# Windowed attention in tiles of 128 tokens of one batch, on small array tiles, with plain values and a new order of issue

## The chip, the cores and the metric

The kernel runs on one core of a Trainium2 chip. Five engines of that core work side by side, each through its own queue in order: TensorE (PE: matrix products; PEld is its loading of weights), VectorE (DVE), ScalarE (ACT), GpSimd (POOL) and SyncE (SP, which here only starts transfers). The metric is device time in microseconds. Before the change it is 1421.82 us, the median of 3 runs (1421.61 to 1422.27).

## The reference

x has 4 batches of 256 tokens with 128 features. Eight layers follow one another: cross attention and feed-forward, four times, each added to x with a gate. The change lies in the first two. The first (L0 cross attention) has 16 heads of 64. The second (L0 feed-forward) is a small transformer of its own, six depths of windowed attention and a gated feed-forward:

```python
for i in range(DEPTH):      # 6
    x = attn_layer(shift_tokens(x), Wqkv[i], q_scale[i], k_scale[i], Wo[i]) + x
    x = ffn_layer(shift_tokens(x), ln_g[i], ln_b[i], W1[i], b1[i], W2[i], b2[i]) + x

def attn_layer(x, Wqkv, qs, ksc, Wo):
    q, k, v = heads(x @ Wqkv)                # 16 heads of 64
    q = l2norm(q) * qs;  k = l2norm(k) * ksc
    q = q * cos * scale + rotate_half(q) * sin * scale
    k = k * cos / scale + rotate_half(k) * sin / scale
    # windows of 32 queries, each with the 64 keys of its own and the previous window
    sim = where(mask, -big, einsum('bhwie,bhwje->bhwij', q, k2) * 8.0)
    out = einsum('bhwij,bhwje->bhwie', softmax(sim), v2)
    return merge(out) @ Wo
```

`shift_tokens` delays the upper 64 features by one token, within a batch. The feed-forward is a layernorm, a product to 2 x 341 columns, a * gelu(gate), and a product back.

## The kernel before

The program has three parts. `front` holds the first layer and the preparation of the weights of depth 0, `l0_ffn` the six depths, `tail` the other six layers. In each, every piece of work has a name, and a list (`ORDER_A`, `ORDER_L0`, `ORDER`) says in which order the pieces are given to the engines, so each engine's order is written out by hand. PSUM has eight banks of 128 x 512; `psum` hands them out in rings by tag (`k.psb`: in `l0_ffn` two for the projections "mm", one each for the other tags). Buffers in SBUF come in rings as well.

Products that must be exact are made of three: a number is split in two parts of type fp32r, high and low, and `mm3` (L274, its three products L276 to L278) adds high x high, high x low and low x high. Other products are float32; one float32 product stands in the profile as two records of TensorE, a transpose as one.

**First layer** (`l0_xattn`, L670). By batch and pair of heads: projections of q and k, scores (`head`, op "s": `mm3` of a head's 64 features on 64 rows of the array, 128 queries, 256 keys, twice), maximum on DVE (L768), exponential on ACT (L774), normalising on POOL (L777), transposes (L784), the product with the values, the output projection.

**Six depths** (`l0_ffn`, L890). A tile of work (`tile_ops`, L1006) is one window of 32 tokens of all 4 batches, so 128 rows; a depth has eight, which follow each other because a window needs the keys and values of the one before. A tile does this:

- `x_in` (L1018 to L1021) gathers the window out of x (`xp`, 4 batches of 257 columns), with the shift, by two copies, and takes the high part; `x_lo` the low part on POOL.
- `tab_d` and `tab_m` load the rotary table of the window and multiply it by the depth's scales.
- `proj` (P): q and k in four groups of 512 columns; `square` and `norm` for the l2 norm; `cos` (L1050), `sin` (L1056), `add` (L1059) for the rotation; `scale` (L1072); `rsqrt_seed` (L878, L879: Ln and Exp on ACT) and `newton` on DVE for the inverse norm.
- `trans` (L1077) transposes, `evac` puts q into a block-diagonal buffer `qbd` (L1084: two heads beside each other, zeros between, each half by its own copy) and k into `kT` (L1087).
- `val`: not the values but the values already multiplied by Wo. `weight_ops` makes these folded weights U for each depth (`mm_u`, L959; `hi_u`, L964; `lo_u`, L967). 16 heads x 128 columns are four groups of 512. `val_e` (L1098) evicts, `val_d` moves them by four transfers each into the layout of keys.
- `score` and `score_h`: a mask product of 128x512 in bf16 (L1118), then 8 products (L1126) with 128 rows of `qbd` and 64 columns, on two column tiles of the array, twice.
- `smax` (L1135), `ssub` (L1138), `sexp` (L1142), `ssum` (L1146), `snorm` (L1151), then transposes (L1157) and their eviction (L1161).
- `out_mm` (L1170): P times folded values, on four column tiles of 32, added up over heads in one bank; `out_e`, one transpose, and `out_r` (L1190) adds x.

**Feed-forward** (`group_ops`, L1206): four groups of 64 tokens x 4 batches a depth, from `fx` (two gathering copies, L1215, L1216) through the layernorm, the six products, Gelu on ACT (with a load of its table before it and of the exponential's after it) and the residual (L1293).

Of the kernel before, what the change touches and what calls it, by code (L numbers as in the profile page):

```python
# [58 lines left out]
def shape_constants():  # L59
# [14 lines left out]
    rot = np.zeros((128, 8, 4, 64), f32)  # L74
    for b in range(4):
        for w in range(8):
            rot[32 * b:32 * b + 32, w] = tabs[:, 32 * w:32 * w + 32].transpose(1, 0, 2)
    i = np.arange(32)
    mask = np.zeros((128, 64), f32)
    prev = np.where(i[None, :] >= i[:, None], 0.0, NEG)  # L80
    cur = np.where(i[None, :] <= i[:, None], 0.0, NEG)
    for b in range(4):
        mask[32 * b:32 * b + 32, :32] = prev
        mask[32 * b:32 * b + 32, 32:] = cur
    sel = np.zeros((18, NMC * 128), f32)
    for e in range(9):
# [6 lines left out]
        "rot": rot.reshape(128, -1), "mask": mask, "sel": sel,  # L93
# [5 lines left out]
def lay_out(inp):  # L99
# [15 lines left out]
    def blockdiag(w):  # L115
        r = np.zeros((8, 128, 2, 128), np.float32)
        w = w.reshape(8, 2, 64, 128)
        r[:, :64, 0] = w[:, 0]
        r[:, 64:, 1] = w[:, 1]
        return c(r.transpose(1, 0, 2, 3).reshape(128, 2048))  # L120

# [3 lines left out]
    o["f_wvT"] = c(W[:, :, 2048:].transpose(0, 2, 1).reshape(6, 8, 128, 128).transpose(0, 2, 1, 3).reshape(6, 128, 1024))  # L125
    o["f_wo"] = np.stack([blockdiag(A("L0_ffn_Wo")[i].reshape(16, 64, 128)) for i in range(6)])
# [103 lines left out]
def ring(k, pool, tag, bufs):  # L230
    """Pools in k.rings hand out the buffers of a tag in turn."""
    if bufs == 1 or pool not in k.rings:
        return tag, bufs
    n = k.turn[pool, tag] = k.turn.get((pool, tag), -1) + 1
    return f"{tag}.{n % bufs}", 1


def psum(k, tag, shape=(128, 512)):
    k.n += 1
    tag = tag if tag in k.psb else "p"  # L240
    tag, bufs = ring(k, k.ps, tag, k.psb[tag])
    return k.ps.tile([128, 512], F32, name=f"ps{k.n}", tag=tag, bufs=bufs)
# [22 lines left out]
def split(k, hi, lo, src, e_hi, e_lo):  # L265
    """hi + lo == src, each in float32r."""
# [14 lines left out]
def rsqrt(k, pool, y, x, tag):  # L281
    """y = x ** -0.5 elementwise for small positive x, by three Newton steps from the exponent's halving."""
# [10 lines left out]
def rstd(k, pool, out, var, eps):  # L293
    """out = (var + eps) ** -0.5 on [128, n] tiles."""
# [5 lines left out]
def ln_group(k, pool, src_tok, nt, eps, want_tok, out_eng=None):  # L300
    """Layernorm without affine of nt token tiles given in PSUM or SBUF [128, nt, 128]."""
# [14 lines left out]
class Flow:  # L316
    """Work in pieces, each with a name; ORDER says in which order the engines get them."""
# [23 lines left out]
def lazy(k, pool, shape, tag, bufs=1, dtype=F32):  # L341
    """A tile taken from its ring by the first piece of work that touches it."""
# [9 lines left out]
def newton_steps(V, y, x, t):  # L352
    """Three Newton steps of y() towards x() ** -0.5."""
# [5 lines left out]
def seed(V, y, x):  # L359
    """y close to x ** -0.5, from the halving of the exponent."""  # L360
# [5 lines left out]
xd.0 as.0 aw.0.0 aw.0.1 aw.0.2 aw.0.3 aw.0.4 aw.0.5 aw.0.6 aw.0.7 aw.0.8 aw.0.9 aw.0.10 an.0 au.0 ch.1 zero ch.0 WKd.0  # L366
WQd.0 WKh.0 cl.0 WKl.0 xd.1 WQh.0 as.1 ah.0 aw.1.0 WQl.0 Dwo aw.1.1 al.0 aw.1.2 bq.0.1 bq.0.0 bh.0.1.0 bh.0.1.1
bl.0.1.0 Dmb bh.0.0.0 wud.0 bh.0.0.1 bl.0.1.1 mb.0 bl.0.0.0 bq.0.3 WVd.0 WVd.1 bh.0.3.0 mb.1 bl.0.0.1 s.0.2 WVh.0
m.0.2.0 s.0.1 aw.1.3 s.0.0 m.0.2.1 m.0.1.0 bh.0.3.1 Dbvrow bl.0.3.1 s.0.3 w2d WVh.1 x.0.2 m.0.1.1 bl.0.3.0 x.0.1 z.0.2
WVl.0 aw.1.4 m.0.0.0 aw.1.5 m.0.0.1 xd.2 wsd bq.0.2 bh.0.2.0 bh.0.2.1 x.0.0 v.0.0.0 wum.0 m.0.3.0 WVl.1 ve.0.0.0 z.0.1  # L370
wuh.0 v.0.1.0 n.0.2 m.0.3.1 t.0.2 wud.2 bl.0.2.1 n.0.1 WKd.1 bl.0.2.0 z.0.0 ve.0.1.0 DxT wul.0 n.0.0 s.0.6 x.0.3
m.0.6.0 aw.1.6 WKh.1 z.0.3 e.0.2 t.0.1 m.0.6.1 WQd.1 s.0.5 t.0.0 WQh.1 WKl.1 m.0.5.0 n.0.3 s.0.4 v.0.0.1 e.0.1 e.0.0
o.0.0 x.0.6 aw.1.7 m.0.5.1 s.0.7 WQl.1 as.2 m.0.4.0 x.0.5 z.0.6 t.0.3 m.0.4.1 bq.0.4 cl.1 aw.2.0 bq.0.5 ve.0.0.1 z.0.5
aw.2.1 x.0.4 m.0.7.0 m.0.7.1 bq.0.6 oe.0.0 bh.0.4.0 aw.1.8 bh.0.4.1 y.0.0 e.0.3 z.0.4 o.0.1 bh.0.5.0 aw.1.9 bl.0.4.0
n.0.5 bl.0.4.1 t.0.5 v.0.1.1 n.0.6 n.0.4 bh.0.6.0 bh.0.6.1 w1d.0 w1h.0 bh.0.5.1 aw.2.2 bl.0.6.0 x.0.7 aw.1.10 aw.2.3
bl.0.5.0 wqd.0 an.1 t.0.6 oe.0.1 bl.0.5.1 bl.0.6.1 aw.2.4 z.0.7 e.0.5 ve.0.1.1 s.0.9 aw.2.5 m.0.9.0 m.0.9.1 e.0.6
t.0.4 aw.2.6 s.0.8 s.0.12 wqd.1 m.0.8.0 m.0.12.0 aw.2.7 n.0.7 e.0.4 m.0.8.1 x.0.9 aw.2.8 v.1.0.0 au.1 xd.3 s.0.10
aw.2.9 ah.1 z.0.9 t.0.7 m.0.12.1 o.0.2 aw.2.10 x.0.8 ve.1.0.0 m.0.10.0 al.1 m.0.10.1 s.0.11 z.0.8 x.0.12 w1l.0 n.0.9
t.0.9 oe.0.2 v.1.1.1 z.0.12 bq.1.0 e.0.7 n.0.8 bq.0.7 wqh.0 e.0.9 x.0.10 m.0.11.0 s.0.13 z.0.10 m.0.11.1 as.3 bh.1.0.0
o.0.3 bq.1.1 ve.1.1.1 bh.0.7.0 aw.3.0 bh.0.7.1 y.0.1 bh.1.0.1 bl.1.0.0 bl.0.7.0 aw.3.1 t.0.8 bl.0.7.1 wql.0 bl.1.0.1  # L380
x.0.11 n.0.12 aw.3.2 t.0.12 aw.3.3 s.0.15 m.0.13.0 bh.1.1.0 e.0.8 n.0.10 aw.3.4 oe.0.3 z.0.11 y.0.2 m.0.13.1 aw.3.5
# [288 lines left out]
def l0_xattn(k, op, pool):  # L670
# [159 lines left out]
    for b in range(4):  # L830
        batch(b)


class Early:
    """The weights of depth 0, prepared in a flow."""

    def __init__(self, op):
# [1610 lines left out]
```

## Time and profile before

| what | value |
|---|---|
| median of the runs | 1421.82 us |
| span of the profiled execution | 1416.4 us (5.4 us of the median lie outside it) |
| PE busy | 1280.0 us, 90%, 11538 matmul records |
| DVE busy | 1162.2 us, 82% |
| ACT busy | 1016.9 us, 72% |
| POOL busy | 799.8 us, 56% |
| first stage, up to | 203 us |
| six depths, up to | 1089 us |

A row for an engine counts the time in which at least one of its instructions runs. Matmuls overlap: an instruction of TensorE lasts some 0.28 us from its start until its last result is written, while the next starts much sooner. What a matmul costs in a busy queue is therefore the spacing of the starts, which the view in order of time shows. The same holds for ACT and DVE to a smaller degree. PEclk is the share of TensorE's full clock that was granted.

### The profile page before, as it was taken

The numbers are of one execution on the slowest core, as the hardware profiler recorded it, in microseconds if no ns is written. First come the engines' busy times: TensorE is split into PE (matmuls) and PEld (weight loads), VectorE is DVE, ScalarE is ACT, GpSimd is POOL, SyncE is SP. The second block draws the span as 40 slices with busy tenths as digits, with TensorE's granted clock in tenths as the row PEclk, the third lists the DMA queues.
The fourth block names the chain that finished last, engine by engine and source line by source line (L and its number), as shares of the span: only waits on it lengthen the run. The fifth ranks groups of instructions, "written<-read, shape, count | busy, mean of one in ns | idle before, by whom it ended". The sixth has DMA issues, their size and how long they took to land. (4 is left out here: it accounts for less than half of the span.)

```text
span 1416.4 us, 32751 instructions
## 1 busy us (share of the span) xinstructions
PE 1280.0 (90%) x11538; PEld 926.2 (65%) x11538; DVE 1162.2 (82%) x3086; ACT 1016.9 (72%) x2408; POOL 799.8 (56%) x987
## 2 busy tenths in 40 slices
PE   5999987889999899999999998999995978899896
PEld 4777755667777677777777766777773733555444
DVE  6867667888899989888899898989864885778777
ACT  5766748888888778888788878888782634446871
POOL 4434547867787867777787777867640111631221
PEclk9999989999999999999999999999996968999676
DMA  5000002234333333333333432332231110201200
GB/s 181 27 20 4 9 17 74 78 80 107 82 93 94 91 84 95 85 88 93 89 102 82 123 83 76 81 89 74 68 74 39 33 47 15 71 0 45 83 1 15
DMA packets 79433, 95.24 MB, mean 67 GB/s; under 512 B 21513, under 2 KB 47793, under 8 KB 79271
## 3 DMA queue, kind: packets, MB, share of 16 engines
q1 hardware_dynamic: 79271, 93.16, 24.5%
q8 instruction: 92, 1.51, 0.5%
q14 instruction: 70, 0.57, 0.1%
HBM read 40.14 MB, written 2.62 MB: 30 GB/s over the span
## 5 line engine op out<-in xcount | busy, mean ns | idle before, releaser
L1126 PEld LDWEIGHTS ps<-fkT,qbd 128*64 128x64 f32 x3072 | 102.7, 138 | 40.4 <-issue 31.7
L1126 PE MATMUL ps<-fkT,qbd 128*64 128x64 f32 (+1 forms) x3072 | 124.1, 227 | 2.4 <-ACT fkT L1087 2.3
L1084 ACT COPY qbd<-ps 64x512 f32<-64x512 f32 x192 | 111.1, 579 | 9.8 <-PE ps L1077 8.3
L777 POOL TENSOR_TENSOR P<-P,pz 128x512 f32<-128x512 f32 x64 | 66.1, 1041 | 86.6 <-DVE pz L776 63.9
L774 ACT ACTIVATE P<-P,pm 128x256 f32<-128x256 f32 x128 | 64.0, 505 | 10.0 <-DVE pm L768 9.7
L768 DVE CUSTOM_DVE_ANT_0 P<-ps,mb 128x256 f32<-128x256 f32 x128 | 50.5, 417 | 22.6 <-PE ps L784 11.2
L2188 ACT ACTIVATE l3P<-ps,l3m 128x256 f32<-128x256 f32 x128 | 58.7, 489 | 10.8 <-PE ps L2207 3.9
L1087 ACT COPY fkT<-ps 128x512 f32<-128x512 f32 x96 | 56.5, 588 | 10.7 <-PE ps L1077 10.4
L1277 DVE SCALAR_TENSOR_TENSOR fge<-ps,cols,fge 114x256 f32<-114x256 f32 x72 | 34.3, 477 | 20.4 <-PE ps L278 10.1
L588 PE MATMUL ps<-ident,ln_xn 128*128 128x128 f32 x72 | 18.9, 340 | 31.8 <-DVE ln_xn L582 31.4
L2179 DVE TENSOR_REDUCE l3m<-ps 128x2 f32<-128x512 f32 x64 | 41.9, 681 | 6.1 <-PE ps L2173 4.3
L725 ACT ACTIVATE qk<-ps,cols 128x256 fp32r<-128x256 f32 x64 | 27.6, 472 | 22.3 <-PE ps L278 21.1
L1270 ACT ACTIVATE fge<-ps,cols 114x256 f32<-114x256 f32 x72 | 34.4, 478 | 9.9 <-PE ps L278 9.2
L588 PEld LDWEIGHTS ps<-ident,ln_xn 128*128 128x128 f32 x72 | 10.3, 158 | 46.8 <-DVE ln_xn L582 21.6
L572 POOL TENSOR_TENSOR ln_h<-ln_x,half 128x2 f32<-128x2 f32 x16 | 3.1, 195 | 66.4 <-DVE ln_x L570 66.0
L276 PE MATMUL ps<-qk 64*128 64x256 f32 x128 | 40.0, 326 | 0.2 <-DVE V L744 0.2
L726 DVE SCALAR_TENSOR_TENSOR qk<-ps,cols,qk 128x256 fp32r<-128x256 f32 x64 | 29.0, 476 | 13.0 <-ACT qk L725 12.9
L784 PE MATMUL ps<-ident,P 128*128 128x128 f32 x256 | 38.4, 279 | 0.4 <-POOL P L777 0.2
L1282 PE MATMUL ps<-fge,fw 114*128 114x256 f32 x144 | 37.2, 395 | 0.7 <-DVE fge L1277 0.7
L1118 PE MATMUL ps<-mk,idb 128*128 128x512 bf16 (+1 forms) x96 | 35.8, 373 | 0.9 <-DVE fP.1_3795_16221 L1138 0.3
L2016 ACT ACTIVATE ma<-ps,cols 128x512 f32<-128x512 f32 x26 | 18.0, 692 | 23.5 <-PE ps L2049 13.6
L277 PE MATMUL ps<-qk 64*128 64x256 f32 x128 | 34.3, 279 | 0.0
(5111 smaller groups left out, 5312.6 us busy)
## 6 DMA issues: line engine op xcount, KB each, us to landing
fwo<-in_f_wo_dram SPq DMA_DIRECT2D x24, 256.0 KB, 3.8
wst<-in_f_wqk_dram SPq DMA_DIRECT2D x24, 256.0 KB, 2.9
fwv<-in_f_wvT_dram SPq DMA_DIRECT2D x24, 128.0 KB, 2.6
w1st<-in_f_w_dram SPq DMA_DIRECT2D x18, 114.0 KB, 2.6
l3K<-dn SPq DMA_DIRECT2D x4, 512.0 KB, 4.0
l3Q<-do SPq DMA_DIRECT2D x8, 256.0 KB, 3.3
wst<-in_m_w_dram SPq DMA_DIRECT2D x6, 256.0 KB, 2.7
fw<-in_f_w_dram SPq DMA_DIRECT2D x6, 171.0 KB
```

Of the source, the lines that this page charges most:

```text
L276: mm(out, lh, rh, start=start, stop=False, **kw)
L768: V.tensor_tensor_reduce(w.P[:, i], w.sp[:, i], mb[:, i], -0.125, 3.0e38, ALU.add, ALU.min, w.m[:, i:i + 1])
L774: nc.scalar.activation(w.P[:, i], w.P[:, i], AF.Exp, scale=-1.0, bias=w.m[:, i:i + 1], accum_out=z()[:, i:i + 1])
L777: op("n", b, h)(lambda: nc.gpsimd.tensor_tensor(w.P, w.P, bc(z().unsqueeze(2), [128, 2, BT]), ALU.mult))
L784: nc.tensor.transpose(w.pt[:, kc, i * 128:(i + 1) * 128], w.P[:, i, kc * 128:(kc + 1) * 128], k.ident)
L1084: nc.scalar.copy(k.qbd[w % 2][r, 4 * j:4 * j + 4, :, par], p[r].rearrange("p (a b t) -> p a b t", a=4, b=4))
L1087: nc.scalar.copy(k.kT[:, s.slot, 4 * jj:4 * jj + 4], p.rearrange("p (a b t) -> p a b t", a=4, b=4))
L1118: nc.tensor.matmul(s4, k.idb, bc(mkv.unsqueeze(1), [128, 8, nb, 32]), start=True, stop=False, skip_group_check=True)
L1126: nc.tensor.matmul(sp[64 * b2:64 * b2 + 64, pr], k.qbd[w % 2][:, pr, 2 * bb + b2].rearrange("p a t -> p (a t)"), k.kT[:, ks, pr, 2 * bb + ...
L1282: nc.tensor.matmul(s.y, d.w2[:, c], s.ge[:, c], start=(c == 0), stop=(c == 2))
L2179: V.tensor_reduce(w.m, w.sp, AX.X, ALU.max, negate=True)
L2188: nc.scalar.activation(P[kc, hp][:, a], w.sp[:, a], AF.Exp, bias=w.m[:, a:a + 1], accum_out=u.z[:, h:h + 1])
```

## The change

The six depths are cut in another way. A tile is now 128 successive tokens (four windows) of one batch; a depth has two for each of four batches. x is kept already shifted, one buffer per batch (`k.X`), so that no gathering is needed, and the feed-forward works on one batch. The order lists are new for the first stage and the six depths; the banks of PSUM are given out by two written lists (`BANKS_A`, `BANKS_L0`) there. `tail` keeps its list.

- Scores: for each of 4 windows, 8 head pairs and 2 heads, one product of 64 rows, 32 queries and 64 keys on a tile of 64x32 of the array; the mask comes from 8 products of 64 rows and 512 columns on the same tiles. Even and odd heads have a bank each.
- The factor 8 is in q's table; the negative maximum is the bias of the exponential, which is one instruction per head (8 for a bank), and the subtraction goes.
- Values are projected plainly (two groups of 512 columns), the folded weights and `mm_u`, `hi_u`, `lo_u` go; PV is 64 products of 64 rows, 64 columns of values and 32 queries on 64x64 tiles, and the output projection follows as eight products (O) after two evictions (Ce).
- The rotary tables stay in SBUF and are multiplied by the scales twice a depth.
- q's transposes are evicted whole, as k's are. A table of ACT is loaded where the function needs another one than was loaded last (`table`).
- In the first stage, the scores of the two heads of a pair are made in turn, on rows 0 to 63 and 64 to 127, in two banks.

```diff
 # l0_xattn
-                    mm3(k, w.sp[:, i], t[r, 0, q], t[r, 1, q], t[r, 2], t[r, 3])
+                    for n, (u, v) in enumerate(((0, 2), (0, 3), (1, 2))):
+                        for j, w in enumerate(sp):
+                            r = slice(64 * j, 64 * j + 64)
+                            nc.tensor.matmul(w.sp[:, i], t[r, u, q], t[r, v], start=(n == 0), stop=(n == 2),
+                                             tile_position=(64 * j, 0), skip_group_check=True)
...
+def table(k, name):
+    if k.table != name:
+        k.table = name
+        k.nc.scalar.preload_act_table_set(name)
...
 # values
-        uh, ul = d.U[hh]
-        mm3(k, s.vp[hh], s.xh, s.xl, uh.rearrange("p r i o -> p (r i o)"), ul.rearrange("p r i o -> p (r i o)"))
+                mm3(k, s.vp[r], xh()[:, ts], xl()[:, ts], d.v[r][0], d.v[r][1])
...
+                for i in range(4):
+                    src = s.vt[r][32 * i:32 * i + 32].rearrange("p (a f) -> p a f", a=8)
+                    nc.sync.dma_start(vu[g]()[cur, i], src)
+                    if g == 0 and i == 0:
+                        nc.sync.dma_start(vu[0]()[nxt, 0], src)
+                    if i < 3:
+                        nc.sync.dma_start(vu[g]()[nxt, i + 1], src)
+                    elif g == 0:
+                        nc.sync.dma_start(vu[1]()[nxt, 0], src)
...
 # scores
-                nc.tensor.matmul(sp[64 * b2:64 * b2 + 64, pr], k.qbd[w % 2][:, pr, 2 * bb + b2].rearrange("p a t -> p (a t)"),
-                                 k.kT[:, ks, pr, 2 * bb + b2], start=False, stop=True, skip_group_check=True,
-                                 tile_position=(0, 64 * b2))
+            for i in range(4):
+                for par in range(2):
+                    r = slice(64 * par, 64 * par + 64)
+                    nc.tensor.matmul(s.sp[par][32 * i:32 * i + 32], k.sel[r, 1 if g == 0 and i == 0 else 0],
+                                     bc(k.mk[r].unsqueeze(1), [64, 8, 64]), start=True, stop=False,
+                                     tile_position=(64 * par, 32 * i), skip_group_check=True)
+            for pr in range(8):
+                for i in range(4):
+                    for par in range(2):
+                        r = slice(64 * par, 64 * par + 64)
+                        c = 128 * g + 32 * i
+                        nc.tensor.matmul(s.sp[par][32 * i:32 * i + 32, pr], qT()[r, pr, 32 * i:32 * i + 32], kT()[r, pr, c:c + 64],
+                                         start=False, stop=True, tile_position=(64 * par, 32 * i), skip_group_check=True)
...
 # softmax
-        V.tensor_tensor(views(s.P[bb])[1], s.sp[bb].rearrange("p h (c m) -> p h c m", c=nb),
-                        bc(s.mx[bb].unsqueeze(2).unsqueeze(3), [128, 8, nb, 32]), ALU.subtract)
-        nc.scalar.activation(views(s.P[bb])[0], views(s.P[bb])[0], AF.Exp, scale=8.0)
+                for pr in range(8):
+                    nc.scalar.activation(P()[:, pr], s.sp[par][:, pr], AF.Exp, bias=mx()[:, pr:pr + 1])
...
 # PV and output projection
-                nc.tensor.matmul(s.y[32 * b:32 * b + 32, :128], s.PT[b // 2][:, g % 2, c, q0:q0 + 32], v[:, b, g],
-                                 start=(g == 0 and c == 0), stop=(g == 3 and c == nb - 1), tile_position=(0, 32 * b),
-                                 skip_group_check=True)
+            s.o = [psum(k, "o").rearrange("p (m q) -> p m q", m=4) for _ in range(2)]
+            for m in range(4):
+                for i in range(4):
+                    q = slice(32 * i, 32 * i + 32)
+                    for par in range(2):
+                        for r in range(2):
+                            kk = slice(64 * r, 64 * r + 64)
+                            nc.tensor.matmul(s.o[r][64 * par:64 * par + 64, m, q], vu[g]()[kk, i, 4 * par + m], s.PT[par]()[kk, m, q],
+                                             start=True, stop=True, tile_position=(64 * r, 64 * par), skip_group_check=True)
+        for r in range(2):
+            op("Ce", l, b, g, r)(lambda r=r: nc.scalar.copy(o()[:, r], s.o[r]))
+            s.y = psum(k, "y")[:, :128]
+            for pr in range(8):
+                nc.tensor.matmul(s.y, d.wo[:, pr], o()[:, pr % 2, pr // 2], start=(pr == 0), stop=(pr == 7))
+            for h in range(2):
+                p, c = halves(h, 128 * g, 128)
+                V.tensor_tensor(u.x1()[p, c], s.y[p], X()[p, c], ALU.add)
...
 # feed-forward
-        nc.vector.scalar_tensor_tensor(d.x2[:, :, c], s.y.rearrange("p (b i) -> p b i", b=4), col(k, "f_b2", l),
-                                       d.x1[:, :, c], ALU.add, ALU.add)
+        for h in range(2):
+            p, c = halves(h, 0, 256)
+            nc.vector.scalar_tensor_tensor(x2()[p, c], s.y[p], col(k, "f_b2", l, 64 * h, 64 * h + 64), x1()[p, c], ALU.add, ALU.add)
```

## The prediction

> **What bounds the kernel now.** The profiled execution spans 1416.4 us; the runs have a median of 1421.82 us, so 5.4 us lie outside the span and are added at the end. First, the busy time of each engine cut at the stage borders: cross attention (15.4 to 203), the windowed attention and feed-forward of six depths (203 to 1089), everything behind it (1089 on). The borders are the waits of TensorE on the layernorm that ends the first stage and on xT (L925).
>
> ```profile
> core 0: us, PE busy (x) PEld busy (x) DVE busy (x) ACT busy (x) POOL busy (x), PEclk, DMA share, GB/s
> 15.40:203.00 187.60, 183.38 (x1240) 139.95 (x1240) 139.49 (x559) 129.70 (x410) 82.04 (x80) 1.00 0.09 28
> 203.00:250.00 47.00, 33.89 (x210) 23.40 (x209) 32.72 (x67) 33.94 (x67) 34.22 (x34) 0.83 0.27 71
> 250.00:1050.00 800.00, 756.12 (x8659) 583.03 (x8660) 717.86 (x1483) 663.10 (x1388) 599.18 (x611) 0.99 0.34 87
> 1050.00:1089.00 39.00, 26.81 (x262) 18.83 (x260) 12.89 (x34) 17.97 (x32) 4.44 (x5) 0.78 0.12 29
> 1089.00:1416.40 327.40, 279.75 (x1171) 160.93 (x1170) 252.33 (x928) 167.15 (x505) 73.30 (x246) 0.81 0.12 37
> ```
>
> Over the six depths (886 us) PE is busy 816.8 us (92%), DVE 763.5 (86%), ACT 715.0, POOL 637.8: PE leads, DVE is close behind. In the first stage PE is busy 98%. PE's waits from 213 to 1064 us sum to 56, the longest 2.5; the time is PE's own instructions. So second, how they follow one another (in order of time: start, length, line, count), since their lengths overlap and the spacing of the starts is what they cost:
>
> ```profile
> 600.28 0.38 PE L1077 MATMUL ps<-ident,fA.1_2053_8534 128*128 128x128 f32 x2
> 600.60 0.69 PE L1126 MATMUL ps<-fkT,qbd 128*64 128x64 f32 x16
> 601.21 0.37 PE L276 MATMUL ps<-fxfh.1_2120_8847,fw1h 128*114 128x256 f32 x1
> 601.42 0.28 PE L277 MATMUL ps<-fxfl.1_2125_8872,fw1h 128*114 128x256 f32 x1
> 601.54 0.28 PE L278 MATMUL ps<-fxfh.1_2120_8847,fw1l 128*114 128x256 f32 x1
> 601.66 0.60 PE L1077 MATMUL ps<-ident,fA.3_2085_8714 128*128 128x128 f32 x4
> ...
> 602.32 0.28 PE L1170 MATMUL ps<-fVU.1_1959_8144,fPT.1_2115_8829 128*32 128x128 f32 x2
> 602.34 0.28 PE L1170 MATMUL ps<-fVU.1_1959_8144,fPT.2_2123_8864 128*32 128x128 f32 x2
> 602.43 0.28 PE L1170 MATMUL ps<-fVU.2_2032_8464,fPT.1_2115_8829 128*32 128x128 f32 x2
> 602.45 0.28 PE L1170 MATMUL ps<-fVU.2_2032_8464,fPT.2_2123_8864 128*32 128x128 f32 x2
> ```
>
> Read from it: a transpose costs 0.109 us. The 16 score records (8 float32 products, two records each) start over 0.46 us, 29 ns each: they come as two column tiles 7 ns apart, each pair 58 ns after the last. The PV records come as four tiles 7 ns apart, four per 0.11 us, 27.3 ns each. The pair of 32-column scores of window 0 also takes 58 ns, so there the 64-column weights set the pace and not the stream. Going into a tiled run costs 0.10 (600.50 would be due, 600.60 is) and 0.05 on its second instruction; coming out 0.10, and 0.09 on the next (601.21 to 601.42 against 0.12 after): 0.33 us a run.
>
> **The change, PE.** Both kernels have 8 tiles of 128 tokens per depth, 48 in all.
>
> Values: the folded products (values times Wo, 4 groups of three 128x512 fp32r) become 2 plain groups: 288 fewer at 0.231 (their starts) = -66.5. The folding itself (L959, 80 records here at 0.216) goes: -17.3.
>
> Scores: before, 64 records at 29 ns and two masks at 0.32 = 2.50 a tile. After, 128 records and 8 short masks on eight tiles of 64x32. If eight run together as two and four did, a round is 58 ns: 16 rounds 0.93, plus one mask round 0.28 = 1.21. 48 x -1.29 = -62.
>
> PV: before 60 records on average at 27.3 ns and one transpose = 1.75. After, 128 records in rounds of four 64x64 tiles, again 64 weight columns, so 58 ns: 1.86; and the output projection, newly its own, 16 records at 0.109 = 1.74. 48 x +1.85 = +89. P's transposes of window 0 double: +2.6.
>
> Runs: the written order of PE enters tiles 277 times in this stage before (159 score runs, 118 PV runs) and 96 times after: -181 x 0.33 = -60. Sum -114: PE 817 to 703.
>
> The unknown is the rate. The trace never shows a long run denser than 27.3 ns a record; after the change one is wanted at 8.9 (scores) and 14.5 (PV). The row: tiles start 7 ns apart inside a round, and the 27.3 is exactly a stream of four (0.109/4). The Trainium skill speaks against it: "TensorE: Matmul & The Clock Gate", section "Wait — 56ns, not 53.3ns?", says that matmul starts never come closer than about 25 ns however narrow they are. By that rule the 264 records a tile cost 6.6 us and not 3.07: 48 x +3.53 = +169, PE 872, a loss. Bounds: 703 and (at 27.3) 901. I take 703, since the 7 ns starts already break 25 where tiles differ; the same page's Part 3 gives about 4 ns between tiles. No run here shows eight at once, or a run of 136.
>
> **DVE.** The subtraction of the maximum (L1138) goes into the exponential: 84 x 0.682 + 12 x 0.417 = -62. The low part of the folded weights: -20 x 0.68 = -14. The residual adds split by partition halves: 24 x 0.477 + 48 x 0.28 = +25; window 0's narrow reductions become wide: +6. 763 to 719.
>
> **ACT**, by starts:
>
> ```profile
> 601.86 0.47 ACT L1270 ACTIVATE fge<-ps,cols 114x256 f32<-114x256 f32 x1
> 602.23 0.59 ACT L1043 ACTIVATE fsq.1_2131_8886<-ps 128x512 f32<-128x512 f32 x1
> 602.71 0.59 ACT L1087 COPY fkT<-ps 128x512 f32<-128x512 f32 x1
> ```
>
> A 512-wide copy is 0.48, a 256-wide with a bias column 0.37. Two value copies a tile less: -46. Transposed q and k: six evictions (four half-partition ones of 0.59) become four of 0.48: -67. The gathers of x (0.85 a tile, and 0.82 per feed-forward) become one 0.30 copy per batch: -54. Folded weights out, value weights in: -4. The 14 table loads at L878 and L879, all between 219 and 296 us: -18. Attention out: one 0.16 copy becomes two of 0.48: +38. Te +3. The exponential: 96 wide ones (-49) become 768 of 64 columns with a bias column. No row has that; the nearest are 0.37 for 256 with bias, less 192 columns at 0.83 ns = 0.21, and 0.136 between starts of the 32-wide frn ones, without bias. "ScalarE: Activation LUTs", section "What ACT_TABLE_LOAD costs", makes it 280 + 53 - 93 = 240 ns. I take 0.21, from PSUM as these are: +161 (the rule: +184; bounds 0.14 to 0.37: +108 to +284). Sum -36: 715 to 679, by the rule 702.
>
> **POOL**: tables multiplied twice a depth and not per tile -26, value weights +13, the rest within 5: 638 to about 627. The value moves on SP's queue stay 16 a tile of the same size; the per-tile table load leaves it.
>
> **First stage.** The two heads of a pair go on two row tiles, alternating, with a bank each. Scores there: 384 records at 0.118 = 45, half if two run together (-22); runs 55 to 25, -10; folding gone, 16 x 0.216, -3.5. PE 183 to 148, DVE 137, ACT 129. Row tiles starting 7 ns apart are seen once before, in the four of L2173 at 1318.99 us.
>
> **From work to time.** Six depths: four engines carry 2933 us in 886, 3.31 at a time; afterwards 2728, at 3.31 that is 824. By the fullest engine alone (DVE 719 at 92%) it is 781. Four engines this even wait on each other more than one that leads, so I stay near the first: 815, -71. First stage: carried work 535 to 496 at 2.85 gives 174; PE alone 151; I take 170, -18. The last stage keeps its order: 0. Span 1416.4 - 89 = 1327, plus 5.4: **about 1333 us**.
>
> **The rivals.** (a) *PE's rate of small matmuls* (ends slower): at 25 ns PE is 872, at 92% 948 us, +62 - 18 = 1466; at 27.3, 979, about 1497. It decides from where PE reaches 832, 92% of the 904 that the first stage's gain pays for: 129 us more than 703, with the 58 and 89 that these records cost in my sum, over 12,672 of them: 21.8 ns each. For it: nothing denser than 27.3 is seen over 64 records. Against: that number is the array's stream. (b) *ACT becomes the bound*: at 0.37 an exponential ACT carries 802, at 92% 872, -14 - 18 = 1390. For: 16 instructions in a row hold two PSUM banks for over 3 us. Against: 0.136 for a 32-wide one. (c) *The saved work returns as waits*: each batch is its own chain now, and transposes, exponentials, POOL's normalising, PV, output projection and feed-forward follow in line; if PE's gaps grow by 100 us (they are 56 from 213 to 1064 now) the six depths take 870 to 890: 1390 to 1420, at worst some us over. If eight tiles run no better than four, PE is +45 (scores 2.14 a tile) and the carried work gives 14 us more: about 1347.
>
> **Chances.** Forecast 0.66 (own range 1300 to 1375); (b) and (c) while still faster 0.11; no change 0.02; slower 0.21, of it 0.17 by (a). A difference of 0.2% (2.8 us) is about what these runs can tell. Faster 0.77, same 0.02, slower 0.21. The range 1300 to 1440 leaves out a little below and most of (a) above.
>
> **What would show it.** Right: scores at 7 to 9 ns between starts in a run, PV at 14 to 15, PE near 700 in the six depths with DVE the fullest, exponentials 0.2 us apart, the first stage ending near 185. Wrong: score and PV starts 20 ns or more apart; ACT over 750; a clock well under 0.99 (it was 0.83 where PE was busy 72%, and I expect 86%).

## The result, and the profile after

The changed kernel takes 1480.64 us (median of 4 runs, 1471.71 to 1483.66) against 1421.71 beside it: 1.041 times as long, 95% interval 1.0375 to 1.0442. The forecast was 1333 us, range 1300 to 1440, with 0.21 for slower. So the sign was wrong, and the time lies outside the range.

The profiled execution of the changed kernel took 1478.0 us and spans 1476.2. Its busy times by stage, with the columns of the table shown for the kernel before:

```profile
core 0: us, PE busy (x) PEld busy (x) DVE busy (x) ACT busy (x) POOL busy (x), PEclk, DMA share, GB/s
17.60:182.00 164.40, 152.10 (x1222) 114.38 (x1222) 130.17 (x541) 127.25 (x409) 81.68 (x80) 0.99 0.09 26
182.00:250.00 68.00, 44.82 (x554) 34.76 (x555) 39.73 (x77) 31.27 (x80) 39.85 (x44) 0.77 0.27 69
250.00:1050.00 800.00, 683.23 (x13909) 581.12 (x13909) 625.18 (x1324) 584.79 (x1574) 548.76 (x567) 0.93 0.29 71
1050.00:1147.00 97.00, 81.08 (x1674) 68.95 (x1673) 64.37 (x149) 64.90 (x172) 44.54 (x46) 0.92 0.16 38
1147.00:1476.20 329.20, 283.80 (x1167) 162.46 (x1166) 250.85 (x923) 167.41 (x505) 73.36 (x246) 0.80 0.12 37
```

The first stage ends near 182 us instead of 203 (forecast 185). The six depths last 965 us (182 to 1147) where they lasted 886 and were forecast at 815. The last stage is about the same. All of the loss is in the six depths, and no engine is fuller there than before: PE 809 us of work in 965 (84%), DVE 729, ACT 681, POOL 633. DVE, ACT and POOL carry what was forecast (719, 679, 627). PE carries 809 instead of 703, and all engines wait more. In the tables below the six depths run from the end of the layernorm wait at about 182 us to the first instruction of TensorE in the last part; by these borders they last 891.8 before and 967.5 after.

What TensorE waits for in the six depths of the changed kernel (us in total, times, longest):

```profile
PE ps L1124 <- issue: 29.9, 21, 2.4
PE ps L1085 <- issue: 12.9, 12, 2.1
PE ps L1124 <- ACT fPT.0_2778_14959 L1110: 6.8, 1, 6.8
PE ps L1029 <- ACT fvt.0_746_2899 L1052: 5.6, 1, 5.6
...
PE ps L274 <- ACT fvt.1_738_2864 L1052: 4.0, 1, 4.0
```

The first two lines are new in kind. L1124 is the PV product and L1085 the score product: TensorE stops *inside* these runs, and "issue" says that it waited for nothing that the profile shows. The kernel before has 2.8 us of waits so marked over its six depths, the changed one 47. One run in the order of time, the PV run at 603.19 (start, length):

```profile
603.19 0.30 PE L1124 MATMUL ps<-fPT.1_1948_10141,fvu.2_1883_9742 64*64 64x32 f32 x4
...
605.25 0.23 PE L1124 MATMUL ps<-fPT.1_1948_10141,fvu.2_1883_9742 64*64 64x32 f32 x2
605.30 0.23 PE L1124 MATMUL ps<-fPT.2_1965_10211,fvu.2_1883_9742 64*64 64x32 f32 x2
605.31 0.23 PE L1124 MATMUL ps<-fPT.1_1948_10141,fvu.2_1883_9742 64*64 64x32 f32 x2
607.85 0.24 PE L1124 MATMUL ps<-fPT.1_1948_10141,fvu.2_1883_9742 64*64 64x32 f32 x1 [2.31 <-issue]
607.85 0.30 PE L1124 MATMUL ps<-fPT.2_1965_10211,fvu.2_1883_9742 64*64 64x32 f32 x4
```

The run is all but done at 605.3, stops, and takes 2.3 us to issue its last five records. Record by record, the rounds of four before the stop begin 58 ns apart (the same pair of tiles at 605.25 and again at 605.31): that is the rate that was disputed.

What ends the pause is in the DMA part of the page: a queue that carries instructions (packets, MB, share of the DMA engines). Before, then after:

```profile
q8 instruction: 92, 1.51, 0.5%
```

```profile
q8 instruction: 147, 2.41, 0.7%
```

Its packets are all of 16,384 bytes. There are 147 of them to 2 x 18,522 = 37,044 matmuls and weight loads, and 92 before to 2 x 11,538; with the 749 instructions of TensorE's sequencer that is 257 to a packet in the changed kernel. So these are TensorE's instructions, in blocks of 256. The places of the pauses confirm it: with TensorE's instructions numbered in the order of their starts, 31 of the 32 pauses of over 0.4 us in the six depths begin at the same place in a block of 256, and the last one two instructions later. The four waits so marked before the change stand 5.7 us or more behind a packet's landing and are of another kind.

A packet of this queue went from 604.83 to 606.40, and TensorE went on 1.45 us later. All 32 pauses end the same way, 1.15 to 1.62 us after a packet has landed and 2.2 to 3.0 us after it started. A block that is used up sooner than the next one comes ends in a pause: of the 34 blocks in the six depths whose 256 instructions started within less than 3 us, 31 were followed by the next instruction over 0.4 us late; of the 83 that took 4 us or more, 2 were. Before the change no 256 successive instructions started within less than 6.4 us. The starts of two packets are never closer than 3.3 us in the changed kernel, and never closer than 7.3 before. What sets these times, no run shows.

The second new wait is ScalarE's. From its waits over the same stretch (a few lines out of many):

```profile
ACT fvt.1_1215_5790 L1052 <- DMA fvu.0_1168_5487<-fvt.1_1196_5596: 6.6, 1, 6.6
ACT fvt.1_828_3400 L1052 <- DMA fvu.0_815_3278<-fvt.1_749_2908: 5.7, 1, 5.7
...
ACT fqkh.2_1093_5104 L933 <- DMA wst.1_1083_5061<-in_f_wqk_dram: 5.5, 1, 5.5
...
ACT fvt.1_2674_14351 L1052 <- DMA fvu.0_2648_14263<-fvt.1_2646_14252: 5.2, 1, 5.2
ACT fvt.1_2776_14942 L1052 <- DMA fvu.2_2760_14881<-fvt.1_2743_14753: 5.1, 1, 5.1
```

L1052 evicts projected values into `fvt`, a ring of two. It must wait until the value transfers of the eviction two earlier have read their buffer. All waits of this kind sum to 57.6 us in 18 times; before the change, to 1.1 us in two. SP's queue shows why, first before, then after (start, length, count):

```profile
614.38 2.43 SPq L1103 DMA_DIRECT2D fVU.1_2181_9124<-fvt.0_2171_9078  x4
618.58 3.38 SPq L1103 DMA_DIRECT2D fVU.1_2181_9124<-fvt.1_2192_9161  x4
624.38 2.41 SPq L1103 DMA_DIRECT2D fVU.1_2181_9124<-fvt.0_2211_9264  x4
```

```profile
608.77 0.54 SPq L1065 DMA_DIRECT2D fvu.2_1981_10321<-fvt.0_1961_10194  x1
609.40 1.47 SPq L1059 DMA_DIRECT2D fvu.1_1980_10312<-fvt.1_1968_10218  x1
610.92 0.58 SPq L1061 DMA_DIRECT2D fvu.1_1980_10312<-fvt.1_1968_10218  x1
611.56 0.58 SPq L1063 DMA_DIRECT2D fvu.1_1980_10312<-fvt.1_1968_10218  x1
612.18 0.59 SPq L1059 DMA_DIRECT2D fvu.1_1980_10312<-fvt.1_1968_10218  x1
```

SP starts one transfer per 0.64 us or so. Before, four in a row belonged to one eviction. Now nine (or seven) do, and a batch issues its four evictions close together, 32 transfers. At that pace seven take 4.5 us and nine 5.8 before the buffer is free, and the next batch's evictions stand behind that, and with them the other work in ScalarE's queue.

### The profile page after: what moved, and what is told of

Read it like the earlier page. It is cut to its first block, busy times and chain, and to the rows that moved or that the text cites. A ratio compares the mean times of both kernels' runs of the same rounds, so it can differ in the third digit from the quotient of the medians.

```text
span 1476.2 us, 47037 instructions
## 1 busy us (share of the span) xinstructions
PE 1245.0 (84%) x18522; PEld 961.7 (65%) x18522; DVE 1117.7 (76%) x3041; ACT 980.5 (66%) x2745; POOL 797.8 (54%) x1000
## 5 line engine op out<-in xcount | busy, mean ns | idle before, releaser
L570 POOL TENSOR_TENSOR ln_h<-ln_x,half 128x2 f32<-128x2 f32 x16 | 3.1, 194 | 69.9 <-DVE ln_x L568 69.5
L786 PEld LDWEIGHTS ps<-ident,P 128*128 128x128 f32 x256 | 28.9, 140 | 13.5 <-POOL P L779 4.3
L809 PE MATMUL ps<-PT,V 128*64 128x256 f32 x256 | 34.5, 391 | 0.6 <-DVE PT L792 0.6
L2200 PE MATMUL ps<-l3Q,l3K 32*128 32x256 f32 x128 | 29.0, 386 | 4.3 <-ACT l3P L2215 3.8
L2200 PEld LDWEIGHTS ps<-l3Q,l3K 32*128 32x128 f32 x128 | 18.7, 229 | 20.2 <-ACT l3P L2215 11.8
L756 PE MATMUL ps<-qk 64*128 64x256 f32 x384 | 30.8, 294 | 0.4 <-DVE qk L723 0.4
L756 PEld LDWEIGHTS ps<-qk 64*128 64x128 f32 x384 | 25.3, 186 | 7.8 <-DVE pm L770 2.2
L2215 ACT ACTIVATION_READ_ACCUMULATOR l3P<-ps,l3m 128x1 f32 x128 | 28.4, 222 | 0.0
L2076 PE MATMUL ps<-ma,mw 128*128 128x512 f32 x52 | 28.0, 631 | 0.1
```

The costliest lines, as they stand in the source:

```text
L756: nc.tensor.matmul(w.sp[:, i], t[r, u, q], t[r, v], start=(n == 0), stop=(n == 2), tile_position=(64 * j, 0), skip_group_check=True)
L786: nc.tensor.transpose(w.pt[:, kc, i * 128:(i + 1) * 128], w.P[:, i, kc * 128:(kc + 1) * 128], k.ident)
L809: nc.tensor.matmul(w.o[64 * hh:64 * hh + 64], vv[kc, h // 8]()[:, (h % 8) * 64:(h % 8 + 1) * 64], PT[h]()[:, kc], start=(kc == 0), stop=(k ...
L2076: nc.tensor.matmul(s.y, k.mw2[:, cs], t.a, start=(c == 0), stop=False)
L2200: nc.tensor.matmul(w.sp[:, a], s.K[r, j0 + a, kc * 128:(kc + 1) * 128], s.Q[r, j0 + a], start=True, stop=True, tile_position=(32 * jj, 0))
L2215: nc.scalar.activation(P[kc, hp][:, a], w.sp[:, a], AF.Exp, bias=w.m[:, a:a + 1], accum_out=u.z[:, h:h + 1])
```

## The experiments

Two theories, then. **F**: TensorE runs dry inside the long runs of small products because its instructions come too late. **V**: ScalarE waits for the value transfers. Their rival is **C**, rival (c) of the prediction: each batch is one chain, and what is saved at one place is waited for at the next. All times are medians; the changed kernel's is 1480.6, and the kernel before, timed beside the runs, took 1420.9 to 1422.4. The other columns are of the one execution that was profiled.

| run | time, us | six depths | pauses "issue" | PE busy | half clock |
|---|---|---|---|---|---|
| before | 1421.7 | 891.8 | 2.8 | 818.8 | 49 |
| changed | 1480.6 | 967.5 | 47 | 809.3 | 165 |
| four value buffers | 1448.5 | 938.5 | 54 | 801.6 | 143 |
| halved runs | 1488.4 | 976.5 | 21 | 828.7 | 147 |
| half as many products | 1409.7 | 902.6 | 0.3 | 738.6 | 145 |
| moves on two queues | 1590.1 | 1079.5 | 34 | 852.0 | 247 |
| same array time | 1418.2 | 909.2 | 0.5 | 773.9 | 124 |
| same array time, four buffers | 1382.4 | 875.4 | 5 | 759.7 | 80 |
| bf16 values, four buffers | 1401.0 | 894.8 | 29 | 744.2 | 140 |
| bf16 values, more room | 1394.7 | 886.0 | 30 | 737.8 | 128 |
| before, PV in halves | 1427.5 | 901.5 | 2.7 | 830.4 | 59 |
| row tiles in turn | 1473.8 | 952.3 | 42 | 792.6 | 126 |

"Half clock" is the time in us within the six depths at which the granted clock was 0.5. "Row tiles in turn" has the changed kernel's code in the six depths: the 15 us, the 17 us of PE busy and the 39 us of half clock between these two lines are what two executions of one code differ by. Smaller differences in these columns say nothing.

**Four value buffers.** The room comes from `ctxT`, which the six depths don't read.

```diff
-                s.vt[r] = sb(k, pool, [128, 512], "fvt", 2)
+                s.vt[r] = sb(k, pool, [128, 512], "fvt", 4)
```

> The changed kernel with a ring of four buffers for evicted values instead of two (room for them comes from ctxT, which is loaded again for the last stage). Theory V (ScalarE waits for the value transfers that SP starts one by one): ScalarE's wait before the value eviction, 57.6 us over the six depths, falls under 15, and the six depths lose 25 to 50 of their 965 us. Theory F (TensorE runs dry inside the long runs of small products because its instructions are not fetched in time): some 30 pauses inside the runs, 47 us, stay, and the six depths change by less than 15 us. Rival C (neither; each batch is one chain, and time saved at one place is waited for at the next): both waits may shrink, the time stays within 10 us.

1448.5 us, ratio to before 1.0195 (1.0158 to 1.0231): 32 us less than the changed kernel, 29 of them in the six depths. Of ScalarE's waits for value transfers one is left:

```profile
ACT fvt.1_749_2908 L1053 <- DMA fvu.1_720_2796<-fvt.1_723_2805: 3.5, 1, 3.5
```

TensorE's pauses inside the runs are as they were:

```profile
PE ps L1125 <- issue: 32.0, 21, 3.7
PE ps L1086 <- issue: 13.0, 11, 1.9
```

Of the 54 us in the table another 5 are a wait before a transpose, not a pause of this kind. So V is a real loss of about 30 us, half of the 57.6 us that the wait lasted, and F is another matter.

**Halved runs.** The last four of the eight head pairs of a score run, and the last two of the four column blocks of a PV run, become pieces of their own, placed behind the next piece of TensorE's work (in 6 of the 48 PV runs nothing of TensorE came to stand between, and they stayed whole).

```diff
-            for pr in range(8):
+            for pr in range(p0, p0 + 4):
...
-            for m in range(4):
+            for m in range(m0, m0 + 2):
```

> The changed kernel with every run of scores and every run of PV products cut in two, with another piece of TensorE's work between the halves (same products, same instructions otherwise, 96 more runs). Theory F: the pauses without a semaphore inside the runs fall from 47 us to under 15, the time at half clock from 163 us towards 100, and against it stand 96 more entries at 0.33 us, 32 us; the six depths lose 20 to 50 us. Theory V: ScalarE's wait for value transfers stays near 58 us and the time grows by 10 to 30 us. Rival C: within 10 us.

The pauses fall by more than half, but not under 15:

```profile
PE ps L1088 <- issue: 11.0, 12, 1.7
PE ps L1132 <- issue: 9.3, 10, 1.9
```

The time does not fall: 1488.4, 8 us more. The blocks used up in under 3 us went from 34 to 25, and those of them with a pause from 31 to 18. Against that stand the ends of some 90 more runs (TensorE's busy time is 19 us longer, hardly more than two executions differ by) and the score reductions, which wait longer for the second half (DVE's wait for L1088: 67 us, where it was 26 for L1085). F's mechanism shows, its gain doesn't; that more work between the halves would bring it was not tried.

**Half as many products.** Each product covers two pairs of heads with the queries of the first, or two windows with the values of the first; the other queries and values are left out.

```diff
-            for pr in range(8):
+            for pr in range(0, 8, 2):
...
-                        nc.tensor.matmul(s.sp[par][32 * i:32 * i + 32, pr], qT()[r, pr, 32 * i:32 * i + 32], kT()[r, pr, c:c + 64],
+                        nc.tensor.matmul(s.sp[par][32 * i:32 * i + 32, pr:pr + 2], qT()[r, pr, 32 * i:32 * i + 32], kT()[r, pr:pr + 2, c:c + 64],
...
-                for i in range(4):
-                    q = slice(32 * i, 32 * i + 32)
+                for i in range(0, 4, 2):
+                    q = slice(32 * i, 32 * i + 64)
```

> The changed kernel with half as many score and PV products, each twice as wide (a pair of heads shares one query block, two windows share one block of values; the other head's queries and the other window's values are left out). The same number of columns streams, with half the instructions: 64 records a run in place of 128. Theory F: the pauses inside the runs vanish (47 us to under 5), the time at half clock falls to near the 43 us of before, and the six depths lose 60 to 110 us. Theory V: ScalarE's wait for value transfers stays or grows, and the six depths lose 0 to 30 us, which shorter runs alone would give. Rival C: under 20 us.

1409.7 us, 0.992 of before (0.989 to 0.995); the six depths lose 65 us and the pauses are gone (0.3 us are left). But the dose was not clean: the shortest score run fell from 1.24 to 0.86 us and the shortest PV run from 1.85 to 0.94, 62 us of array time over 48 runs of each. And the time at half clock hardly fell. Hence "Same array time" below.

**Moves on two queues.**

```diff
                     if i < 3:
-                        nc.sync.dma_start(vu[g]()[nxt, i + 1], src)
+                        nc.scalar.dma_start(vu[g]()[nxt, i + 1], src)
```

(and the two other copies to the next window likewise)

> The changed kernel with the half of the value transfers that go to the next window started from ScalarE's queue instead of SP's. Theory V: the wait of ScalarE before the value eviction falls from 57.6 us to under 20, the weights behind the transfers come earlier, and the six depths lose 20 to 50 us less what ScalarE pays for 384 starts. Theory F: the pauses inside the runs stay at 47 us and the six depths change by less than 15. Rival C: within 10 us, or slower by the starts on ScalarE.

1590.1 us, 110 more. The value eviction waits 10.7 us instead of 57.6. But each start now holds ScalarE's own queue, for 0.51 to 2.2 us, median 0.60: 267 us for the 384 of them, and in 218 of these ScalarE did nothing. Its waits in the six depths grew from 278 to 388 us, the longest ahead of other evictions:

```profile
ACT fo.0_1798_9154 L1128 <- DMA fvu.0_1795_9128<-fvt.1_1778_9017: 7.3, 1, 7.3
ACT fo.0_1890_9780 L1128 <- DMA fvu.2_1883_9742<-fvt.1_1874_9651: 6.8, 1, 6.8
```

The profile puts these down to the last transfer before them. The timeline shows that the first is nine starts in a row; the last five and the eviction behind them (start, length, count):

```profile
592.85 0.60 ACTq L1061 DMA_DIRECT2D fvu.0_1795_9128<-fvt.1_1778_9017  x1
593.49 1.88 ACTq L1063 DMA_DIRECT2D fvu.0_1795_9128<-fvt.1_1778_9017  x3
595.42 0.60 ACTq L1065 DMA_DIRECT2D fvu.1_1796_9137<-fvt.1_1778_9017  x1
596.06 1.07 ACT L1128 COPY fo.0_1798_9154<-ps 128x512 f32<-128x512 f32 x2 [7.31 <-DMA fvu.0_1795_9128<-fvt.1_1778_9017]
```

This says nothing for or against V; it shows what the starts cost on a queue that has other work.

**Same array time.** Half as many instructions again, but each product so wide that a run streams about as long: 32 score products of 192 columns, 32 PV products of 128 queries. Half of the heads' queries and half of the windows' values are left out.

```diff
-            for pr in range(8):
+            for pr in (0, 2, 4, 5):
...
-                        nc.tensor.matmul(s.sp[par][32 * i:32 * i + 32, pr], qT()[r, pr, 32 * i:32 * i + 32], kT()[r, pr, c:c + 64],
+                        nc.tensor.matmul(s.sp[par][32 * i:32 * i + 32, pr:pr + 3], qT()[r, pr, 32 * i:32 * i + 32], kT()[r, pr:pr + 3, c:c + 64],
...
-                for i in range(4):
-                    q = slice(32 * i, 32 * i + 32)
+                for i in (0, 2):
+                    q = slice(0, 128)
```

> The changed kernel with half as many score and PV products, each so much wider that the streamed time of a run stays about what it was: 32 score products of three heads' keys (192 columns) in place of 64 of 64 columns, 32 PV products of 128 queries in place of 64 of 32. (Half of the heads' queries and half of the windows' values are left out.) It separates what the run before it mixed, fewer instructions and less array time. Theory F (instructions not fetched in time): the pauses inside the runs fall from 47 us to under 5 and the six depths lose 40 to 70 us of 968, though runs at full clock last about as long as before, 1.2 to 1.8 us. If array time was what made half as many products quicker, the six depths lose under 15. Theory V (value transfers): ScalarE's wait of 57.6 us stays.

1418.2 us, 62 less than the changed kernel, 58 of them in the six depths. The shortest runs last 1.16 and 1.71 us (1.24 and 1.85 in the changed kernel), which accounts for 11 us over 48 tiles. Half clock falls from 165 to 124 us, but by no more than two executions of one code differ. TensorE's waits over the six depths hold one line of this kind:

```profile
PE ps L1029 <- issue: 0.5, 1, 0.5
```

No 256 successive instructions now start within less than 3.0 us. So some 50 us of the loss is the number of instructions in a dense run, not the time of the array. In the six depths the pauses fell by 47 us and TensorE's busy time by 35, while its other waits rose by 24: a part of what was saved did come back as waits. ScalarE's waits for value transfers stayed at 53 us.

**Same array time and four buffers.** The edits of "Same array time" and of "Four value buffers" together.

> Both causes taken away at once: half as many products of equal streamed time, and four buffers for evicted values. If F and V are two separate losses, they add: 29 us of the buffers and 40 to 70 of the instructions, six depths at 870 to 900 us. If each only uncovers the other's wait (theory C, the chain of a batch), the six depths end within 10 us of the better of the two alone. At 815 us, the forecast, nothing else would be missing; what is over 815 is left for the clock and the chain.

1382.4 us, 0.9728 of before (0.9702 to 0.9755). The two gains add: 32 and 62 alone, 98 together. C predicted no more than the better of the two, and falls as the cause of these losses. The 5 us marked "issue" are one wait before a transpose, 10 us after a packet, and not a pause inside a run.

```profile
182.20:1057.60 875.40, 759.66 (x9991) 618.74 (x9991) 738.48 (x1582) 676.61 (x1823) 633.99 (x658) 0.95 0.29 75
```

So without the two losses the change is worth about 39 us, not 89 (in a kernel that leaves out half of the scores' queries and of PV's values): 875 us in the six depths and not some 820.

**Before, PV in halves.** Does the number of instructions cost, or their density? Each PV product of the kernel before is issued as two halves of 64 columns (the sums that come out are not the reference's).

```diff
+            for f in (slice(0, 64), slice(64, 128)):
...
-                nc.tensor.matmul(s.y[32 * b:32 * b + 32, :128], s.PT[b // 2][:, g % 2, c, q0:q0 + 32], v[:, b, g],
+                    nc.tensor.matmul(s.y[32 * b:32 * b + 32, f], s.PT[b // 2][:, g % 2, c, q0:q0 + 32], v[:, b, g, f],
```

> The kernel before, with each of its PV products (128 columns) issued as two of 64: the same streamed columns, 2880 more records, 5760 more instructions, all inside its many short runs. Theory F in its sharper form (blocks of 256 instructions reach TensorE no closer than 3.3 us apart, so only a dense stretch of more than that many runs dry): the blocks of the kernel before are at least 7.3 us apart, the new runs are still short, so no pauses appear (issue under 5 us in the six depths) and the time stays within 12 us of 1421. If what costs is the number of instructions as such (55 more blocks cost the changed kernel 47 us of pauses), some 23 more blocks cost about 20 us of pauses and the time grows by 20 or more.

```profile
q8 instruction: 115, 1.88, 0.5%
```

```profile
PE ps L1077 <- issue: 2.7, 4, 1.5
```

23 more blocks and not one new pause; 1427.5 us, 1.0043 of before (1.0019 to 1.0067), and PE's busy time is 12 us longer. Density it is: its PV runs have at most 128 records, half of them 32, its quickest block of 256, by the division found above, takes 2.7 us, and no two packets start closer than 3.7 us.

**Row tiles in turn.** The first layer's scores, with the loop over the two heads outside the one over the three products:

```diff
-                    for n, (u, v) in enumerate(((0, 2), (0, 3), (1, 2))):
-                        for j, w in enumerate(sp):
+                    for j, w in enumerate(sp):
+                        for n, (u, v) in enumerate(((0, 2), (0, 3), (1, 2))):
```

> The changed kernel with the scores of the first layer issued head after head (three products on one row tile, then three on the other) in place of alternating between the two tiles. If two row tiles running together is what the first stage gained by, it goes from 164 back by 15 to 22 us, and the whole by as much, 1495 to 1503 us. If the gain came from fewer runs and the folding that went, under 5 us.

1473.8 us, with the first stage unchanged (PE busy 152.4 us in 17.6 to 182, where it was 152.1). It looks as if the two row tiles gave nothing. The timeline says otherwise (start, length, count):

```profile
100.67 0.87 PE L756 MATMUL ps<-qk 64*128 64x256 f32 x10
```

Ten records in the space of 0.87 us, and single starts come in pairs 10 ns apart, a pair per 0.11 us, though the kernel gives them three by three: twelve records start within 0.71 us, as they did by turns (0.70). The two tiles still ran together, so the run did not do what it was built for. The share of this concurrency in the first stage was not measured by a run of its own; the rows give it (below). The 7 us between the medians lie in the six depths, whose code is the same: executions of the changed kernel differ by as much.

**A version that beats both.** PV in bf16 halves the instructions of a PV run and its array time, and values in bf16 take half the room, so that four buffers fit. Attention weights and values are then rounded to bf16: a lower precision than both kernels have.

```diff
-                s.vt[r] = sb(k, pool, [128, 512], "fvt", 2)
+                s.vt[r] = sb(k, pool, [128, 512], "fvt", 4, BF)
...
-    vu = [lazy(k, pool, [128, 4, 8, 64], "fvu", 3) for _ in range(2)]
+    vu = [lazy(k, pool, [128, 4, 8, 64], "fvu", 3, BF) for _ in range(2)]
...
-            PT = s.PT[par] = lazy(k, pool, [128, 4, 128], "fPT", 3)
+            PT = s.PT[par] = lazy(k, pool, [128, 4, 128], "fPT", 3, BF)
```

> The changed kernel with the PV product in bf16 (weights of attention and values rounded to bf16, so a different precision) and four buffers for values, which in bf16 take the room of two. A bf16 product is one record where a float32 one is two: 64 records a PV run, half the instructions and half the array time. Theory F: pauses inside PV runs go, those inside score runs (13 us) stay; theory V: ScalarE's wait goes. Both together: the six depths lose 70 to 110 us of 968, and the whole falls to 1370 to 1410, below the kernel before. Theory C: 29 to 45 us, 1435 to 1450.

1401.0 us, 0.9859 of before (0.9824 to 0.9893), inside what was expected. One part of the expectation failed: the pauses in PV runs did not go.

```profile
PE ps L1124 <- issue: 12.8, 10, 1.9
PE ps L1085 <- issue: 12.7, 14, 1.6
```

A bf16 run has half the instructions but lasts as little as 0.51 us where the float32 run took 1.85, so it is nearly twice as dense. The run of the same count over 1.71 us never paused: this too says density.

Then the room that is left:

```diff
-    vu = [lazy(k, pool, [128, 4, 8, 64], "fvu", 3) for _ in range(2)]
+    vu = [lazy(k, pool, [128, 4, 8, 64], "fvu", 4, BF) for _ in range(2)]
...
-        qT = lazy(k, pool, [128, 8, 128], "fqT", 2)
+        qT = lazy(k, pool, [128, 8, 128], "fqT", 3)
...
-                s.vt[r] = sb(k, pool, [128, 512], "fvt", 2)
+                s.vt[r] = sb(k, pool, [128, 512], "fvt", 6, BF)
```

> The kernel with PV in bf16 and four buffers (1401 us), with the room that bf16 frees given to rings: six buffers for evicted values, four for their layout by keys, three for the transposed queries. Theory V: the value transfers no longer hold anything up there (3.8 us are left), so nothing is gained: within 6 us of 1401. Theory C: a batch held back by buffers of the one before would come earlier, and the six depths lose 8 to 20 us.

1394.7 us, 0.9806 of before (0.9773 to 0.9838), and 9 us less in the six depths. That leans to the side of C, but the two intervals overlap and executions of one code differ by more: a hint, no more.

## Why the prediction was wrong

**The disputed rate was right.** In a full-clock PV run a round of four takes 58 ns, 14.6 a record (forecast 14.5); the shortest score run has 128 records in 1.24 us, 9.7 each (forecast 8.9, "7 to 9"). The rule of the Trainium skill that the prediction weighed, no starts closer than about 25 ns, does not hold across tiles: the measurement decides against it, and against rival (a). It named the right place, small matmuls, and the wrong reason.

**What failed first: the step that counted instructions only by their time on the array.** "Runs: the written order of PE enters tiles 277 times in this stage before (159 score runs, 118 PV runs) and 96 times after: -181 x 0.33 = -60" made long runs a pure gain. The step took no account of where 128 records, 256 instructions with their weight loads, come from within 1.3 or 1.9 us. The Trainium skill has this, in "Runtime: NRT & Kernel Launch", section "Instruction fetch mechanics": instructions are refilled in 16 KiB blocks of 256. The trace agrees (16,384 bytes a packet). The section calls the cost mostly hidden, since fetching is faster than issue; here the trace differs: a block came 2.2 to 3.0 us after its packet had started, the pauses sum to 47 us, and a score run with its masks uses up 272 instructions in 1.5 us. By the page's word the term is 0, by the runs 50 to 62 us. The queue's packets were on the page of the kernel before (92, against 11,538 records), so that the count would rise by half could have been worked out. That the pauses would be this long could not: the densest 256 instructions of that trace took 6.4 us and no pause followed.

**Second: "The value moves on SP's queue stay 16 a tile of the same size", costed at nothing.** The count is right. What moved is their grouping: nine to an eviction in place of four, 32 to a batch in one place of the order, through the same ring of two. Before, other work stood between the groups of four; when it went, ScalarE stood behind the transfers for 57.6 us. It cost 32 us.

**Third: PE's 703, even where nothing pauses.** From start to start, without the waits, the score runs and their masks take 88 us (forecast 58), the PV runs 122 (89), and the other lines' instructions at half clock 101 (34 before). Nearly half of the 106 us is the clock: instructions at half clock hold 130 us where they held 35, and half of the difference is 47 (95 us and 30 in the execution of "row tiles in turn", the same code here). The spells are multiples of 3.41 us, mostly one, and begin on a grid of that length. Laid on this grid, they follow idle time. Of the windows at full clock in which TensorE did nothing for less than 0.9 us, 1 of 178 was followed by half clock in the changed kernel; of those with 1.8 us or more, 19 of 21. Over all twelve traces it is 3 of 2238 and 184 of 191 (and 77 of 402 in between). So pauses that add up to half a window are paid again in the 3.41 us after it. The Trainium skill has the clock fall after an idle window of about 3.4 us ("TensorE: Matmul & The Clock Gate", Part 1); the length of the spells agrees, but here about half a window was enough, whatever the wait was for. In "half as many products" half clock stayed: its other waits sum to 166 us, where they were 110. No experiment moved the clock by itself.

**Work to time.** "Four engines at 3.31 at a time" came out as 3.21 without the two losses (2809 us of work in 875). At 3.31 it would have been 849, against a forecast of some 820 by these borders: of the 55 us, about half is more work and half less overlap. Rival (c) was thus partly right: TensorE's waits other than "issue" rose from 71 us to 110, and are still 112 with both losses gone. (Its own figures, six depths of 870 to 890 us, come to 1388 to 1408 and not to 1420.)

**What was right.** The first stage: -20 (forecast -18). The projections and scores there took 95.8 us from start to start before and 69.9 after; the 384 score records, in pairs on two row tiles, take 29 us of it, where one tile at 0.118 each would need 45. DVE, ACT and POOL came within 10 us; for ACT that is in part luck, since its exponentials came out some 10 us under their term and the others as much over theirs. The 64-column exponentials start 0.196 us apart (forecast 0.21; 0.24 by the Trainium skill's reckoning in the prediction), and ACT was never the bound:

```profile
589.31 1.75 ACT L1098 ACTIVATE fP.1_1933_10077<-ps,fmx.0_1926_9995 128x64 f32<-128x64 f32 x8
590.87 1.82 ACT L1098 ACTIVATE fP.2_1935_10090<-ps,fmx.1_1929_10003 128x64 f32<-128x64 f32 x8
```

Of the signs that "would show it", the rates, the exponentials and the first stage came as for right. PE did not come near 700 and was fuller than DVE, and the sign on the other side that came was the clock: 0.93 in the middle of the stage where 0.99 stood before.

## What to carry to other kernels

When a change cuts products small, count TensorE's instructions in the densest stretch, not only their time: here blocks of 256 instructions that were used up in under 3 us ended in a pause in 31 of 34 cases, most often of 1 to 2.5 us, while 5760 more instructions in short runs cost no pause. When an unchanged number of transfers is regrouped, ask how long the buffer they read is held, and who stands behind its next writer. And a forecast that relies on a long unbroken run of one engine should say what feeds that run.

## What the runs showed of the hardware that was not expected

- TensorE's instructions arrive in packets of 16,384 bytes, 256 instructions, that take about 1.1 us; in the changed kernel their starts are at least 3.3 us apart, and after a pause TensorE goes on 1.15 to 1.62 us after the landing. "Issue" inside a run of one line, always at the same place of a block, is how it shows.
- The clock fell by windows of 3.41 us: to half after 184 of 191 windows in which TensorE was idle for 1.8 us or more, and after 3 of 2238 with less than 0.9.
- Two row tiles ran together even when each got three products in a row: pairs 10 ns apart. Whether they start out of the written order, or reached TensorE in another, the trace does not tell.
- Eight tiles of 64x32 start 3.3 ns apart and sustain 9.7 ns a record, so a round of eight takes 78 ns on average, not the 58 of two or four.
- Starting 384 transfers from ScalarE's queue cost 110 us: each start held the queue 0.51 to 2.2 us, and for 218 of these 267 us ScalarE did nothing.
